# A gate on each unit's attention, a batch's rotation over two MLPs, and TensorE in written order up to the first MLP

## The chip, the cores and the metric

The kernel runs on one core of one Trainium2 chip, in float32. The metric is the device time of one execution in microseconds (us), the median of several runs. Engine names in the profile: PE is TensorE (PEld its weight loads), DVE VectorE, ACT ScalarE, POOL GpSimd, SP the engine that issues most DMAs.

## The reference

Two layers on `x` (8 batches, 512 tokens, 576 channels) with one conditioning row per batch. The first rotates each token in a 64-dimensional subspace: `U` from a QR of `P`, a rotation `R` from the matrix exponential of a skew matrix. The second is a transformer block whose attention runs over the 16 heads of each single token, not over tokens.

```python
U, _ = jnp.linalg.qr(P)
R = expm(skew(silu(cond) @ W.T + b))            # per batch, 64 x 64
z = x @ U
x = x + (z @ R - z) @ U.T

shift_a, scale_a, gate_a, shift_m, scale_m, gate_m = split(silu(c) @ ada_w + ada_b, 6)
qkv = modulate(layernorm(x), shift_a, scale_a) @ qkv_w + qkv_b      # 576 -> 3 * 576
attn = softmax(einsum('nthd,ntkd->nthk', q * 36**-0.5, k))          # 16 x 16 heads, per token
out = einsum('nthk,ntkd->nthd', attn, v).transpose(0, 2, 1, 3).reshape(n, t, d)
x = x + gate_a * (out @ proj_w + proj_b)
h = gelu(modulate(layernorm(x), shift_m, scale_m) @ fc1_w + fc1_b)  # 576 -> 2304
x = x + gate_m * (h @ fc2_w + fc2_b)
```

The transpose before the reshape mixes tokens: a tile of 128 tokens of attention becomes another set of rows for the projection, so attention goes out to DRAM (`att_d`) and comes back (`at`).

## The kernel before

Work is cut into 16 **units**: unit k is one batch and two of its four tiles of 128 tokens, `units[k] = (b, (0, 1))` or `(b, (2, 3))`.

A preparation of some 240 us computes the modulations, the QR and the exponential. Then these pieces follow one another for each unit:

- `rotation(b)` gives six pieces for a batch: `project_z(0)`, `rotate(0)`, `rotate(1)`, `project_z(1)`, `rotate(2)`, `rotate(3)`. `project_z` loads `xT`, multiplies it (`zps`, L730) and ScalarE copies it out; its first call also makes `gz`. `rotate` loads `xt`, multiplies (`rot`, L741), VectorE adds the product (L749), SP stores the result (`xr`), and `normed` computes the layernorm: statistics on VectorE (L137 to L139), the root on GpSimd (L140), the scaling on VectorE (L141).
- `feature_major(b, half)` transposes two normed tiles (`htr`, L773); ScalarE applies the modulation (`hT`, L777).
- `qkv(b, i)` gives six token groups of a tile: ten matmuls each (`qkvp`, L800), ScalarE's copy to `qs` (L811, three buffers) and ScalarE's DMA to `tok_d` (L812). The first two tiles stay on chip.
- `attention(b, ts)` is a generator, all on VectorE but the exponential: it loads the tokens (`qkv <- tok`, L825, three buffers), and for each tile forms the scores in four pairs of a product (L834) and a reduction (L841), subtracts the maximum, takes the exponential on ScalarE (L848), divides by the sum, and multiplies by the values in four more pairs (L862, L869). SP stores each tile to `att_d` (L871).
- `Projection`: SP loads weights, `at` (L902) and `x1`. `turn(t)` transposes `at` (`atr`, L913) and ScalarE copies it to `aT` (L914). `product(t, n)` multiplies (`pj`, L924); VectorE multiplies by the gate into `pt` (L926) and adds it (L927). `norm` is the second layernorm, `turn_normed` transposes (`h2tr`, L942) and ScalarE modulates (`h2T`, L945).
- `mlp`: nine groups of `fc1` (L969) with the gelu on ScalarE (L977), GpSimd's sums (`ss`, `s3`, L1025 to L1028) and the second layer's matmuls (L1040 to L1045), then `p7` (L1055), then VectorE's closing operations (L1065 to L1080, L984). A dictionary `aside` names pieces to be issued ahead of a group.

The main loop for unit k runs: the projection of unit k, with up to 12 token groups of a unit three ahead between its steps (`ahead`; two tiles per unit up to k = 10, then one); the MLP of unit k, with, for every first half of a batch, all six rotation pieces and both `feature_major` of batch b + 2 aside; then what is left of the attention of unit k + 1; and the generator for unit k + 2 is made.

What sets the order: outside `manual_schedule` a planner reorders each engine's instructions, by the program's order as priority and by its own estimate of when operands are ready, and then each engine works through its list in order. So VectorE may take up a later unit's attention as early as the planner saw its tokens, however late it stands in the program. The preparation has the written order on all engines. From there to the end of the first projection (`held`, closed at k = 0), GpSimd and VectorE have the written order, and TensorE, ScalarE and SP are planned. After that all are planned.

PSUM: `ps_mm` has two banks, shared by `zps`, `rot`, `htr`, `qkvp` and `pj`; `ps_f1` has two, for `fc1`, `atr`, `h2tr` and `p7`; `ps_acc` four.

Of the kernel before, what the change touches and what calls it, by code (L numbers as in the profile page):

```python
# [9 lines left out]
F32 = mybir.dt.float32  # L10
# [7 lines left out]
B, S, D = 8, 512, 576  # L18
R = 64
H, DH = 16, 36  # L20
# [4 lines left out]
HALF = D // 2  # L25
# [23 lines left out]
def rotate_then_dit_block(  # L49
# [16 lines left out]
    nc = tc.nc  # L66
# [36 lines left out]
    def srows(c):  # L103
        return 65 if c == 4 else 128
# [6 lines left out]
    small = ctx.enter_context(tc.tile_pool(name="small", bufs=4))  # L111
# [38 lines left out]
    engines = {mybir.EngineType.PE, mybir.EngineType.DVE, mybir.EngineType.Activation, mybir.EngineType.Pool}  # L150
    sc = const.tile([128, NK, B], F32, tag="sc", name="sc")
    with tc.manual_schedule(engines=engines), tc.tile_pool(name="prep", bufs=1) as prep, tc.tile_pool(name="qrs", bufs=2) as qrs, tc.tile_pool(
        name="ada", bufs=4
    ) as adap, tc.tile_pool(name="exs", bufs=1) as exs, tc.tile_pool(
        name="ps_qr", bufs=1, space=PSUM
    ) as ps_qr, tc.tile_pool(
        name="ps_ex", bufs=2, space=PSUM
    ) as ps_ex, tc.tile_pool(name="ps_m", bufs=2, space=PSUM) as ps_m, tc.tile_pool(
        name="ps_x", bufs=1, space=PSUM
# [374 lines left out]
        t, done = column_products(0), None  # L534
        for j in range(R):
            t, done = qr_step(j, t, done)
# [13 lines left out]
        if True:  # L550
# [131 lines left out]
            for h in range(2):  # L682
                p = slice(h * R, (h + 1) * R)
# [3 lines left out]
    tiles = ctx.enter_context(tc.tile_pool(name="tiles", bufs=2))  # L687
# [8 lines left out]
    def gate_rows(which, b):  # L696

        g = big.tile([128, D], F32, tag=f"gate{which}", name=f"gate_{which}_{b}")
        nc.sync.dma_start(out=g, in_=gates_d[which, b : b + 1, :].to_broadcast([128, D]))
        return g  # L700
# [86 lines left out]
    def qkv(b, i):  # L787


        hT = hTs[b]  # L790
        stay = b == 0 and i < 2
        if stay:
            tok = toks[b, i] = tiles.tile([128, 3 * D], F32, tag="qkv", name=f"qkv_{b}_{i}", bufs=3)

        def group(n):
            cols = slice(n * HALF, (n + 1) * HALF)
            ps = ps_mm.tile([128, HALF], F32, tag="mm", name=f"qkvp_{b}_{i}_{n}")
            for c in range(NK):
                k = srows(c)
                nc.tensor.matmul(  # L800
                    ps,
                    lhsT=hT[0:k, c, i * 128 : (i + 1) * 128],
                    rhs=wqkv[0:k, c, cols],
                    start=c == 0,
                    stop=c == NK - 1,
                )
            if stay:
                nc.scalar.copy(tok[:, cols], ps)
            else:
                qs = tiles.tile([128, HALF], F32, tag="qs", name=f"qs_{b}_{i}_{n}", bufs=3)  # L810
                nc.scalar.copy(qs, ps)  # L811
                nc.scalar.dma_start(out=tok_d[b][i * 128 : (i + 1) * 128, cols], in_=qs)  # L812

        return [lambda n=n: group(n) for n in range(6)]

    def attention(b, ts):


        HC = 4
        hb = f"{b}_{ts[0]}"  # L820
        own = []
        for i in ts:
            if (b, i) not in toks:
                toks[b, i] = tiles.tile([128, 3 * D], F32, tag="qkv", name=f"qkv_{b}_{i}", bufs=3)
                nc.sync.dma_start(out=toks[b, i], in_=tok_d[b][i * 128 : (i + 1) * 128])  # L825
            own.append(toks.pop((b, i)))
        sc = [small.tile([128, H, H], F32, tag="sc", name=f"sc_{hb}_{t}", bufs=3) for t in range(2)]

        def scores(t):
            q = own[t][:, 0:D].rearrange("p (h d) -> p h d", d=DH)  # L830
            k = own[t][:, D : 2 * D].rearrange("p (h d) -> p h d", d=DH)
            for c in range(H // HC):
                pr = tiles.tile([128, HC, H, DH], F32, tag="pr", name=f"qk_{hb}_{t}_{c}", bufs=1)
                nc.vector.tensor_tensor(  # L834
                    pr,
                    q[:, c * HC : (c + 1) * HC].unsqueeze(2).to_broadcast([128, HC, H, DH]),
                    k.unsqueeze(1).to_broadcast([128, HC, H, DH]),
                    ALU.mult,
                )
                yield  # L840
                nc.vector.tensor_reduce(sc[t][:, c * HC : (c + 1) * HC, :], pr, AX.X, ALU.add)  # L841
                yield

        def raised(t):
            mx = small.tile([128, H], F32, tag="mx", name=f"mx_{hb}_{t}", bufs=2)
            nc.vector.tensor_reduce(mx, sc[t], AX.X, ALU.max)
            nc.vector.tensor_tensor(sc[t], sc[t], mx.unsqueeze(2).to_broadcast([128, H, H]), ALU.subtract)
            nc.scalar.activation(sc[t], sc[t], AF.Exp, scale=DH**-0.5)  # L848

        def shares(t):  # L850
            sm = small.tile([128, H], F32, tag="sm", name=f"sm_{hb}_{t}", bufs=2)
            nc.vector.tensor_reduce(sm, sc[t], AX.X, ALU.add)
            nc.vector.reciprocal(sm, sm)
            nc.vector.tensor_tensor(sc[t], sc[t], sm.unsqueeze(2).to_broadcast([128, H, H]), ALU.mult)

        def values(t):
            i = ts[t]
            v = own[t][:, 2 * D :].rearrange("p (d h) -> p d h", h=H)
            att = tiles.tile([128, H, DH], F32, tag="att", name=f"att_{hb}_{t}")
            for c in range(H // HC):  # L860
                pr = tiles.tile([128, HC, DH, H], F32, tag="pr", name=f"pv_{hb}_{t}_{c}", bufs=1)
                nc.vector.tensor_tensor(  # L862
                    pr,
                    sc[t][:, c * HC : (c + 1) * HC, :].unsqueeze(2).to_broadcast([128, HC, DH, H]),
                    v.unsqueeze(1).to_broadcast([128, HC, DH, H]),
                    ALU.mult,
                )
                yield
                nc.vector.tensor_reduce(att[:, c * HC : (c + 1) * HC, :], pr, AX.X, ALU.add)  # L869
                yield  # L870
            nc.sync.dma_start(  # L871
                out=att_d[b][:, i * 128 : (i + 1) * 128, :].rearrange("h t d -> t h d"), in_=att
            )


        yield from scores(0)
        raised(0)
        yield from scores(1)
        raised(1)
        shares(0)  # L880
        yield from values(0)
        shares(1)
        yield from values(1)
# [206 lines left out]
    units = [(b, (i, i + 1)) for b in range(B) for i in (0, 2)]  # L1090
    N = len(units)

    def now(pieces):
        for piece in pieces:
            if piece:
                piece()

    def ops(n, of):
        for _ in range(n):
            next(of, None)  # L1100

    first, second = rotation(0), rotation(1)
    held = ctx.enter_context(ExitStack())
    held.enter_context(tc.manual_schedule(engines={mybir.EngineType.Pool, mybir.EngineType.DVE}))
    first[0]()
    feature_major(0, 0)
    q = qkv(0, 0)
# [6 lines left out]
    q = qkv(0, 1)  # L1114
    att = attention(*units[0])
# [31 lines left out]
    feature_major(1, 1)  # L1147
    now(qkv(1, 2))
    q = qkv(1, 3)
    now(q[:3])  # L1150
    ops(4, att)
    next_sums()
    ops(40, att)
# [1 line left out]
    att = attention(*units[1])  # L1155
    ops(6, att)

    ahead = {0: q[3:]}
    tiles_of = [(unit[0], i) for unit in units[4:] for i in unit[1]]
    for k in range(1, N - 1):  # L1160
        for tile_ in [tiles_of.pop(0) for _ in range(2 if k < 11 else 1)]:
# [3 lines left out]
    for k, (b, ts) in enumerate(units):  # L1165
        if ts[0] == 0:
            gate_a, gate_m = gate_rows(0, b), gate_rows(1, b)
            gb2 = big.tile([128, D], F32, tag="gb2", name=f"gb2_{b}")
            nc.sync.dma_start(out=gb2, in_=fc2_b.to_broadcast([128, D]))
            nc.gpsimd.tensor_tensor(gb2, gb2, gate_m, ALU.mult)  # L1170
        pr = Projection(b, ts, gate_a)
        q = ahead.get(k, [])
        if k:
            q = [piece for tile_ in q for piece in qkv(*tile_)]

        q = [None] * (12 - len(q)) + q
        now(q[:5])
        pr.turn(0)
        now(q[5:6])
        pr.product(0, 0)  # L1180
        pr.turn(1)
        now(q[6:7])
        pr.product(0, 1)
        pr.norm(0, gb2)
        now(q[7:8])
        pr.product(1, 0)
        now(q[8:9])
        pr.product(1, 1)
        pr.norm(1, gb2)
        if k == 0:  # L1190
            ops(1, att)
        now(q[9:11])
        pr.turn_normed((0, 1))
        now(q[11:])
        pr.turn_normed((2, 3))
        pr.turn_normed((4,))
        if k == 0:
            held.close()
        aside = {}
        if ts[0] == 0 and b + 2 < B:  # L1200
            p = rotation(b + 2)
            aside = {1: p[0], 2: p[1], 4: p[4], 5: p[5]}
            aside[3] = lambda two=p[2:4]: now(two)
            aside |= {7: lambda: feature_major(b + 2, 0), 8: lambda: feature_major(b + 2, 1)}
        mlp(pr, gate_m, aside)
        ops(40, att)
        if k + 2 < N:
            att = attention(*units[k + 2])


# [49 lines left out]
```

## Time and profile before

| | |
|---|---|
| median of 3 runs | 2232.36 us (2232.07 to 2233.22) |
| the profiled execution | 2232.94 us, span 2231.2 us |
| busy, share of the span | TensorE 94%, VectorE 81%, ScalarE 19%, GpSimd 31% |
| mean granted clock of TensorE | 0.956 |
| DMA | 400.79 MB, 180 GB/s in the mean |
| TensorE busy in 400 to 1300 us, per 100 us | 94.3 to 99.0 |
| VectorE busy in 400 to 1300 us, per 100 us | 94.6 to 99.4 |
| VectorE busy in 1700 to 2100 us, per 100 us | 45.5 to 64.4 |
| chain that ended last | TensorE 45%, VectorE 33%, issue 11% |

How to read it: a span is one execution from its first instruction to its last. Busy time of an engine counts instructions that run, its waits are listed apart, each put down to the one event that came last. Lines L... are those of the kernel before. The granted clock is 1 at full speed and 0.5 at half. The first 240 us are the preparation, where the clock is at half for long stretches; the change does not touch it.

### The profile page before, as it was taken

How to read it: one execution, taken by the hardware profiler on the slowest of the kernel's cores; microseconds unless marked ns; L12 is line 12 of the kernel's file. 1: busy time of each engine (PE TensorE's matmuls, PEld its weight loads, DVE VectorE, ACT ScalarE, POOL GpSimd, SP SyncE). 2: the span in 40 equal slices, each digit the busy share in tenths (PEclk: the TensorE clock that was granted, in tenths of full speed). 3: DMA queues.
4: the chain of work that ended last, by engine and by line, in shares of the span. 5: the costliest groups of instructions: out<-in, count | busy, mean ns of one | idle time of the engine just before them, and what ended most of it. 6: DMA issues, size and time to landing. Idle time of an engine off the chain costs nothing.

```text
span 2231.2 us, 27868 instructions
## 1 busy us (share of the span) xinstructions
PE 2099.5 (94%) x10087; PEld 1681.0 (75%) x10087; DVE 1812.8 (81%) x2530; ACT 428.2 (19%) x916; POOL 687.8 (31%) x918
## 2 busy tenths in 40 slices
PE   6996998999999999999999998999999999999988
PEld 3475776787878787787778787887878788887867
DVE  8898598799999999999999997979879526742930
ACT  2232221212121121212122121212122111111110
POOL 2331233332324133333324132322313323332422
PEclk9855898999999999999999999999999999999999
DMA  8202365483848567575657566575756665765654
GB/s 268 84 2 73 101 210 141 148 265 126 262 143 256 161 188 216 163 214 178 206 177 236 157 188 190 192 208 168 206 186 198 196 209 185 206 206 177 198 175 125
DMA packets 239789, 400.79 MB, mean 180 GB/s; under 512 B 85502, under 2 KB 127435, under 8 KB 239652
## 3 DMA queue, kind: packets, MB, share of 16 engines
q1 hardware_dynamic: 213732, 372.46, 55.1%
q10 hardware_dynamic: 25920, 26.55, 3.7%
q8 instruction: 80, 1.31, 0.2%
q14 instruction: 57, 0.47, 0.1%
HBM read 340.01 MB, written 58.94 MB: 179 GB/s over the span
## 4 chain that ended last, share of the span: by engine, by line
PE 45%; DVE 33%; issue 11%; POOL 5%; DMA 3%; ACT 2%; SPq 0%; ACTq 0%; POOLq 0%; DVEq 0%
PE fc L969 15%; PE qkvp L800 8%; DVE pv L862 6%; DVE att L869 6%; DVE qk L834 6%; DVE sc L841 6%; PE fc L1040 5%; PE fc L1045 3%; PE pj L924 3%; PE fc L1042 2%; PE p L1055 2%; DMA qkv<-tok 1%; PE ada L352 1%; PE zps L730 1%; PE dp L270 1%
## 5 line engine op out<-in xcount | busy, mean ns | idle before, releaser
L969 PE MATMUL fc<-h2T,w 128*128 128x256 f32 (+1 forms) x2880 | 652.7, 381 | 7.3 <-ACT h2T L945 7.1
L969 PEld LDWEIGHTS fc<-h2T,w 128*128 128x128 f32 (+1 forms) x2880 | 539.6, 191 | 83.4 <-ACT h2T L945 12.1
L800 PE MATMUL qkvp<-wqkv,hT 128*128 128x288 f32 (+1 forms) x1920 | 490.8, 409 | 7.0 <-ACT qs L811 4.4
L800 PEld LDWEIGHTS qkvp<-wqkv,hT 128*128 128x128 f32 (+1 forms) x1920 | 362.5, 191 | 109.7 <-ACT qs L811 6.2
L834 DVE TENSOR_TENSOR qk<-qkv 128x2304 f32<-128x2304 f32 x128 | 334.5, 2613 | 70.4 <-DMA qkv<-tok 62.0
L862 DVE TENSOR_TENSOR pv<-sc,qkv 128x2304 f32<-128x2304 f32 x128 | 335.2, 2618 | 2.2
L1025 POOL TENSOR_TENSOR ss<-gt 128x128 f32<-128x128 f32 x144 | 133.7, 929 | 637.8 <-ACT gt L977 637.8
L869 DVE TENSOR_REDUCE att<-pv 128x144 f32<-128x2304 f32 x128 | 325.7, 2545 | 2.5
L841 DVE TENSOR_REDUCE sc<-qk 128x64 f32<-128x2304 f32 x128 | 325.7, 2544 | 2.1
L977 ACT ACTIVATE gt<-fc 128x512 f32<-128x512 f32 x144 | 86.0, 598 | 652.5 <-PE fc L969 652.2
L811 ACT COPY qs<-qkvp 128x288 f32<-128x288 f32 x180 | 71.9, 400 | 531.4 <-PE qkvp L800 489.6
L1045 PEld LDWEIGHTS fc<-wt,ss 128*128 128x128 f32 x1152 | 161.6, 191 | 15.3
L1040 PE MATMUL fc<-wq,gt 128*128 128x288 f32 x576 | 163.4, 405 | 2.8 <-ACT gt L977 2.8
L1045 PE MATMUL fc<-wt,ss 128*128 128x144 f32 x1152 | 165.6, 287 | 0.0
L140 POOL TENSOR_TENSOR rstd_m<-rstd_m,mhalf 128x1 f32<-128x1 f32 x32 | 30.6, 956 | 357.6 <-DVE rstd_m L139 353.6
L1040 PEld LDWEIGHTS fc<-wq,gt 128*128 128x128 f32 x576 | 107.5, 189 | 26.4 <-ACT gt L977 3.7
L1071 DVE TENSOR_TENSOR u<-u,fc 128x288 f32<-128x288 f32 x16 | 7.2, 449 | 147.9 <-ACT u L1070 146.8
L924 PE MATMUL pj<-w2q_p,aT 128*128 128x288 f32 x384 | 110.1, 424 | 17.3 <-DVE pt L926 12.7
L1027 POOL TENSOR_TENSOR ss<-gt,ss 128x128 f32<-128x128 f32 x144 | 109.0, 757 | 11.2
L985 POOL TENSOR_TENSOR x<-x,mt 128x288 f32<-128x288 f32 x64 | 51.0, 797 | 187.7 <-DVE mt L984 187.7
L924 PEld LDWEIGHTS pj<-w2q_p,aT 128*128 128x128 f32 x384 | 73.1, 195 | 43.8 <-DVE pt L926 17.2
L926 DVE TENSOR_TENSOR pt<-pj,gate 128x288 f32<-128x288 f32 x64 | 28.8, 450 | 91.0 <-PE pj L924 91.0
(253 smaller groups left out, 2416.6 us busy)
## 6 DMA issues: line engine op xcount, KB each, us to landing
w<-in_fc_w SPq DMA_DIRECT2D x288, 320.0 KB
wq<-in_fc_q SPq DMA_DIRECT2D x144, 432.0 KB
wt<-comb_d SPq DMA_DIRECT2D x144, 432.0 KB
tok<-qs ACTq DMA_DIRECT2D x180, 144.0 KB
qkv<-tok SPq DMA_DIRECT2D x30, 864.0 KB
w2q_p<-in_proj_w SPq DMA_DIRECT2D x32, 432.0 KB
xT<-in_x_t SPq DMA_DIRECT2D x16, 640.0 KB
xt<-in_x SPq DMA_DIRECT2D x32, 288.0 KB
```

Source lines behind the costliest of these rows:

```text
L800: nc.tensor.matmul(ps, lhsT=hT[0:k, c, i * 128 : (i + 1) * 128], rhs=wqkv[0:k, c, cols], start=c == 0, stop=c == NK - 1,)
L834: nc.vector.tensor_tensor(pr, q[:, c * HC : (c + 1) * HC].unsqueeze(2).to_broadcast([128, HC, H, DH]), k.unsqueeze(1).to_broadcast([128, H ...
L841: nc.vector.tensor_reduce(sc[t][:, c * HC : (c + 1) * HC, :], pr, AX.X, ALU.add)
L862: nc.vector.tensor_tensor(pr, sc[t][:, c * HC : (c + 1) * HC, :].unsqueeze(2).to_broadcast([128, HC, DH, H]), v.unsqueeze(1).to_broadcast( ...
L869: nc.vector.tensor_reduce(att[:, c * HC : (c + 1) * HC, :], pr, AX.X, ALU.add)
L924: nc.tensor.matmul(ps, lhsT=aT[0:k, c, :], rhs=w, start=c == 0, stop=c == NK - 1)
L969: nc.tensor.matmul(ps[:, k], lhsT=w1[0:n, c, :], rhs=h2T[0:n, c, 0 : NU * 128], start=c == 0, stop=c == NK - 1,)
L977: nc.scalar.activation(gt.rearrange("p k t s -> p (k t s)"), ps.rearrange("p k s -> p (k s)"), AF.Gelu)
L1025: nc.gpsimd.tensor_tensor(ss[:, 0], gt[:, 0, 1], gt[:, 1, 1], ALU.add)
L1027: nc.gpsimd.tensor_tensor(ss[:, 2], gt[:, 1, 0], ss[:, 1], ALU.subtract)
L1040: nc.tensor.matmul(p[k], lhsT=whole[k][0], rhs=whole[k][1], start=g == 0, stop=stop)
L1045: nc.tensor.matmul(bank[:, side], lhsT=lhs, rhs=rhs[:, n * QUARTER : (n + 1) * QUARTER], start=False, stop=stop, skip_group_check=True,)
```

## The change

- `attention` takes a function `after`; if there is one, the first VectorE instruction of the unit's attention copies one column of what it returns into the first score tile. The loop hands over `pr.aT[0]`. The function is called when the generator first runs, one turn of the loop later, so `pr` is then the projection of the unit before: attention of unit j reads `aT[0]` of unit j - 1. This holds from unit 2 on.
- The six rotation pieces of batch b + 2 and its two `feature_major` are shared by the MLPs of the two units of batch b, three and one in each, before groups 1, 3, 5 and 8.
- `held` includes TensorE, which has the written order until the end of the first projection. The last tile's token groups before the loop are two, not three, and those in the first projection are placed one by one.
- `qs` has four buffers in place of three, `sc` two in place of three.

```diff
-                qs = tiles.tile([128, HALF], F32, tag="qs", name=f"qs_{b}_{i}_{n}", bufs=3)
+                qs = tiles.tile([128, HALF], F32, tag="qs", name=f"qs_{b}_{i}_{n}", bufs=4)
...
-    def attention(b, ts):
+    def attention(b, ts, after=None):
...
-        sc = [small.tile([128, H, H], F32, tag="sc", name=f"sc_{hb}_{t}", bufs=3) for t in range(2)]
+        sc = [small.tile([128, H, H], F32, tag="sc", name=f"sc_{hb}_{t}", bufs=2) for t in range(2)]
+
+        if after is not None:
+            nc.vector.tensor_copy(sc[0][:, 0, 0:1], after())
...
-    held.enter_context(tc.manual_schedule(engines={mybir.EngineType.Pool, mybir.EngineType.DVE}))
+    held.enter_context(tc.manual_schedule(engines={mybir.EngineType.PE, mybir.EngineType.Pool, mybir.EngineType.DVE}))
...
     q = qkv(1, 3)
-    now(q[:3])
+    now(q[:2])
...
-    ahead = {0: q[3:]}
+    ahead = {0: [None] * 5 + q[2:3] + [None] * 3 + q[3:]}
...
         aside = {}
-        if ts[0] == 0 and b + 2 < B:
-            p = rotation(b + 2)
-            aside = {1: p[0], 2: p[1], 4: p[4], 5: p[5]}
-            aside[3] = lambda two=p[2:4]: now(two)
-            aside |= {7: lambda: feature_major(b + 2, 0), 8: lambda: feature_major(b + 2, 1)}
+        if b + 2 < B:
+            if ts[0] == 0:
+                coming = rotation(b + 2)
+            p = coming[:3] if ts[0] == 0 else coming[3:]
+            aside = {1: p[0], 3: p[1], 5: p[2], 8: lambda: feature_major(b + 2, ts[0] // 2)}
         mlp(pr, gate_m, aside)
         ops(40, att)
         if k + 2 < N:
-            att = attention(*units[k + 2])
+            att = attention(*units[k + 2], after=lambda: pr.aT[0][:, 0, 0:1])
```

## The prediction

> **What bounds the kernel.** I read the page's busy line first, then busy time in stretches cut where TensorE starts `turn` of each unit (T0 to T15, from the timeline: T0 368, T1 510, T2 625, T11 1735, T12 1833, T13 1932, T14 2030, T15 2129), then the waits, then the timeline around TensorE's largest gaps.
>
> ```profile
> span 2231.2 us, 27868 instructions
> PE 2099.5 (94%) x10087; PEld 1681.0 (75%) x10087; DVE 1812.8 (81%) x2530; ACT 428.2 (19%) x916; POOL 687.8 (31%) x918
> ```
> ```profile
> 1257.00:1368.00 111.00, 111.00 (x525) 92.24 (x524) 109.56 (x70) 20.38 (x38) 32.48 (x40) 1.00 0.66 193
> 1368.00:1502.00 134.00, 126.75 (x582) 102.56 (x581) 108.91 (x115) 27.23 (x51) 41.63 (x53) 0.97 0.65 198
> 1735.00:1833.00 98.00, 96.40 (x462) 80.84 (x461) 35.03 (x45) 15.15 (x28) 28.28 (x44) 1.00 0.66 204
> ```
> After the stretch, columns are its length, then busy time of PE, PEld, DVE, ACT, POOL, then the granted clock. From 400 us on TensorE never rests long, whether VectorE is full (111) or a third full (98), so it sets the end. No matmul is added or removed; all there is to win is TensorE's gaps. Added up from the timeline (over 0.3 us), they are 50 us between 400 and 2120, and 17 us between 344 and 369.
>
> ```profile
> PE pj L924 <- DVE pt L926: 12.7, 9, 4.6
> PE fc L1042 <- POOL ss L1027: 7.0, 6, 2.5
> PE atr L913 <- DMA at<-att: 6.0, 2, 5.2
> PE zps L730 <- DVE xt L749: 5.7, 4, 3.2
> DVE qk L834 <- DMA qkv<-tok: 62.0, 7, 13.0
> ```
> Columns: total us, times, longest. The last line explains part of the first. From unit 7 on VectorE has caught up with its supply: it starts a unit's attention as soon as the projection stage three units ahead has made its tokens, and stands in front of their load. What is queued behind it stands too, such as `pt`, which must empty the PSUM bank that TensorE wants next (VectorE, then TensorE, at unit 10's projection):
>
> ```profile
> 1621.67 0.46 DVE L137 BATCH_NORM_STATS2 st_m<-x 128x6 f32<-128x288 f32 x1
> 1629.07 2.56 DVE L834 TENSOR_TENSOR qk<-qkv 128x2304 f32<-128x2304 f32 x1 [6.94 <-DMA qkv<-tok]
> 1631.54 0.45 DVE L926 TENSOR_TENSOR pt<-pj,gate 128x288 f32<-128x288 f32 x1
> ```
> ```profile
> 1632.05 3.25 PE L924 MATMUL pj<-w2q_p,aT 128*128 128x288 f32 x6 [3.63 <-DVE pt L926]
> 934.85 4.64 PE L730 MATMUL zps<-xT,u 128*128 128x256 f32 x10 [3.23 <-DVE xt L749]
> 348.82 5.17 PE L800 MATMUL qkvp<-wqkv,hT 128*128 128x288 f32 x10 [4.07 <-ACT qs L811]
> 368.24 0.90 PE L913 MATMUL atr<-ident,at 128*128 128x128 f32 x3 [5.23 <-DMA at<-att]
> ```
> A gap costs more than itself: six `pj` matmuls took 3.25 us here, 1.62 elsewhere, because the clock fell to half:
>
> ```profile
> 931.00:945.00 14.00, 10.77 (x38) 8.53 (x37) 12.83 (x13) 2.25 (x3) 1.40 (x4) 0.76 0.52 167
> 1628.00:1641.00 13.00, 8.88 (x25) 6.05 (x24) 11.90 (x11) 0.80 (x2) 0.31 (x1) 0.74 0.30 91
> ```
> Ten matmuls after the gap took 4.96 us, start to start, against 2.43: 2.5 per drop. There are four in mid-kernel: after gaps of 3.24, 3.63 and 4.60, and after 2.08 and 2.28 that lie 2 us apart. [...]
>
> **Part 1, the gate.** A unit's attention may start only when the unit before it has `aT[0]`. It binds everywhere: even the latest starter was early (unit 2's attention began at 487.5, T1 was 510).
> - Removed: the head-of-line wait for tokens. They are now made two units before use. The gaps of 4.60 (1388) and 3.63 (1628) go, with 2 x 2.5 of clock: -13. What is late next is the ordinary `pt` wait behind one 2.55 us attention operation (0.3 to 1.2 us in units 1 to 3), which was there already.
> - Moved: the two exponentials of a unit. In before they drift to the end of an MLP, where the change of ScalarE's table (1.28 us, twice) holds up the last gelu: gaps at 1102 to 1107 (0.68 + 2.49) and 1231 to 1237 (2.08 + 2.28 + 2.3 of clock), and three of 0.5 to 0.7. After the gate they sit some 25 and 50 us behind `turn`, in the projection and the first MLP groups, where TensorE has a group queued. 11.7 at stake; I take -8 (bounds -11.7 and +3, if the early groups pay what three ends of MLPs paid).
> - Added: 14 copies of 128x1; nearest row 0.15 us (`rstd`, 128x1). On VectorE, outside TensorE's chain: 2 us of slack. Behind the waiting copy are queued attention and `pt`; `pt` needs a product that TensorE computes after that same `aT`, so no one else waits.
> - Added: VectorE loses its lead. From `aT[0]` to the attention's end it needs 16 pairs of 5.19 us (83.0), the softmax steps 4.3 and the projection's own operations 7.6, so 95; the last MLP's closing operations push its start to about +3. At the end of the kernel a store and a load hand it over: last reduce done 2128.86, `turn(1)` 2137.65, so 8.8. Ready: 3 + 95 + 1 of joints + 8.8 = 107.8 after `turn`. TensorE comes to `turn(1)` after its own period plus 6 (turn 1.1, two products 4.9). Units 1 to 11 have a period of 122.5 ((1735 - 510) / 10); with half a rotation (5.2) the attention is ready at 113, wanted at 128.5: covered. Units 12 and 13 have 98.4: wanted at 104.4, late by 3.4 plus 2.3 of clock, unless its six token groups (2.43 each) are ordered ahead. Bounds 0 and +11.4; I take +6. Unit 15 does not change: its second tile is made at k = 14 in both (loaded 2065.6).
>
> **Part 2, the shared rotation.** `project_z(1)` no longer follows a `rotate` in the same MLP, where both PSUM banks still waited for VectorE's `xt`: gaps 1.52, 0.77 and 3.24 and 2.2 of clock, 7.7; I take -7. Each MLP now gets one x load, two `rotate` and one `feature_major`; the four x and xr DMAs of a half are spread on SP's queue, and the two normed tiles are held from group 3 to 8, against four before. Tokens for the next batch are still made one unit after `feature_major`. Bounds -7.7 and +3 (an early `rotate` that waits for its load).
>
> **Part 3, TensorE in written order until the first MLP, and four `qs`.** The planned order is nearly the written one up to 362 us. Then the planner put `turn(0)` of unit 0 ahead of nine token groups, and it waited 5.23 us, at half clock until 372. Written: five transposes, eight groups, `turn(0)`, one group, `product(0, 0)`. From 361.9 to 394.9 lie 33 us; the work at full clock is 22 for nine groups, 3 for transposes and 1 for the turn, so 26: -7. The next three products have no groups between them, as now (394.9 to 405, no gap). `turn(1)` needs the second tile, ready at about 378 by the 8.8 above, wanted at about 388. The fourth `qs` puts off the stall at 344.8 by one group, 2.43, if its cause (ScalarE stood 8 us in front of a store) stays; -1 of it. Smaller `sc` costs nothing: in-order VectorE has finished with the old tile first. Together -8 (bounds -17, all gaps there; +5, a written instruction that waits where the planner had a filler).
>
> **Sum.** -13 - 8 + 6 - 7 - 8 = -30. Counted another way: units 1 to 3 show what a projection loses when nothing special happens, 3.1, 4.2 and 2.3. Fifteen units at 2.5 make 37 where now 50 and 9 of clock are lost: -22, with the start and the late units -24. I take -28. The profiled execution took 2232.9 (1.7 more than its span; 0.6 above the median): 2204.9, less the 0.6: **2204**.
>
> **Rivals.**
> - *The gate comes too late (slower).* If VectorE's order puts the copy behind the projection's last norm, some 25 us after `turn`, attention is ready 22 us later. Units 12 and 13 then wait 25 us each and 2.3 of clock, the ten others about 1.5 and some clock (20): +75, with -34 of gains: about 2270. It decides once attention starts more than 15 us after `aT[0]`. For: the projection is earlier in the program. Against: at units 1 to 3 attention pairs are planned between the projection's operations. 13%.
> - *The gaps move (no change).* Now every projection coincides with a starting attention; if each loses unit 2's 4.2 us, 14 make 59, all that was removed; the start's -8 goes against the late units' +6: 2222 to 2240, middle 2231. For: a new plan is drawn for everything after the first projection. 19%.
> - *The start loses*: written order waits 5 us, the rest holds: 2217. 5%.
> - *Cleaner than thought*: all units like 7 and 9 (0 and 1.4): 2180. 10%.
> - *GpSimd is blocked.* Its `s` takes 0.456 us in the median and 2.85 at most, when a VectorE product runs. Late MLPs, now free of attention, get it: up to 2.4 a group, nine groups, units 11 to 14: +86, 2290. A saturated MLP (unit 1's) lost only 0.65 to it, so 3%. [...]
> - That the gate never binds is excluded by the 487.5 above.
>
> **Numbers.** The forecast (2192 to 2222) has 50%. A measurement here can tell about 0.2%, 4.5 us. Faster: 50 + 10 + 5 + 5 of "the gaps move" = 70%; same 8; slower 13 + 3 + 6 = 22. The range 2184 to 2246 leaves out half of the cleaner case, most of the late gate and GpSimd: 19%.
>
> **What would show it.** Right: `qk <- DMA qkv<-tok` under 20 us; no `pj` gap over 2 us; no `zps <- xt`; `at<-att` at the first `turn` gone; attention starting within 5 us of each `aT[0]`; VectorE near 95% busy in 1735 to 2030. Wrong: gaps of over 5 us ahead of `turn(1)` at units 13 and 14, `atr <- DMA at<-att` growing to tens of us, new half-clock stretches, or TensorE waits before 400 us that were not there.

## The result, and the profile after

| | before | after |
|---|---|---|
| median, runs of the same chip | 2232.79 us (2232.07 to 2239.58) | 2208.88 us (2205.87 to 2213.21) |
| profiled execution, span | 2232.94, 2231.2 us | 2205.87, 2204.2 us |
| mean granted clock | 0.956 | 0.961 |

The ratio is 0.9888, 95% interval [0.9862, 0.9913]: faster by 1.1%. Line numbers below are those of the kernel after, or of an experiment's own kernel; in the kernel after, most lines stand 4 further down than before.

The page's span, busy line and the new group of copies:

```profile
span 2204.2 us, 27929 instructions
PE 2090.5 (95%) x10087; PEld 1679.3 (76%) x10087; DVE 1801.2 (82%) x2544; ACT 434.9 (20%) x922; POOL 714.1 (32%) x918
L831 DVE COPY sc<-aT 128x1 f32<-128x1 f32 x14 | 2.1, 152 | 109.4 <-ACT aT L918 109.4
```

TensorE has as many instructions as before and is busy 9 us less, at a mean clock of 0.961 for 0.956. The 14 copies cost 2.1 us and wait 109.4 us. The waits show where:

```profile
DVE sc L831 <- ACT aT L918: 109.4, 10, 11.0
DVE qk L838 <- DMA qkv<-tok: 8.6, 1, 8.6
PE qkvp L800 <- DVE pt L930: 15.0, 14, 1.8
PE h2tr L946 <- DVE xm L141: 6.4, 5, 3.5
PE fc L1046 <- POOL ss L1031: 3.2, 6, 0.9
PE atr L917 <- DMA at<-att: 2.8, 1, 2.8
```

Ten of the 14 copies wait, 11 us each; the other four, of units 12 to 15, don't. The wait for tokens is down from 62.0 us to 8.6, `zps` no longer waits for `xt`, and no `pj` waits for `pt`. That last wait has not gone but moved: it is now `qkvp` that meets it, 14 times, 1.8 us at most.

In stretches (after length, busy time of PE, PEld, DVE, ACT, POOL, then granted clock), one middle unit and one late one:

```profile
1095.00:1215.00 120.00, 118.18 (x554) 96.48 (x553) 98.45 (x89) 24.06 (x45) 39.95 (x47) 1.00 0.66 193
1788.00:1893.00 105.00, 100.50 (x462) 82.97 (x461) 95.63 (x75) 17.95 (x31) 32.47 (x45) 0.97 0.67 189
```

In the middle TensorE lost 1.8 of 120 us, with VectorE idle for 21.55. In the late unit, unit 12, it lost 4.5 of 105, and VectorE is at 91%. In the same unit before, TensorE lost 1.6 of 99, and VectorE was at 75% (36% in units 11 and 13):

```profile
1833.00:1932.00 99.00, 97.40 (x468) 81.53 (x467) 74.38 (x60) 15.16 (x28) 33.51 (x44) 1.00 0.66 199
```

To see where the 27.0 us of the two spans came from, I cut both at the starts of the MLPs (first `fc<-h2T` of each unit in the timeline). Stretch k runs from the start of MLP k to that of MLP k + 1 and so holds the projection of unit k + 1. Gaps are TensorE's, over 0.3 us:

| stretch | before | after | difference | gaps before, after |
|---|---|---|---|---|
| start to MLP 0 | 414.9 | 412.0 | -3.0 | 11.3, 11.6 (from 240 us) |
| 0 to 9 | 1243.2 | 1195.1 | -48.1 | 43.8, 14.0 |
| 10 to 14 | 493.5 | 517.2 | +23.7 | 13.7, 25.0 |
| MLP 15 to the end | 79.6 | 80.0 | +0.4 | none |

The middle won 48 us. 30 are gaps. Some 11 are clock: four half-clock stretches of 6.8 us, in which TensorE was busy for 21.7 us in all, half of it lost. 3.2 are no gain: two `rotate` pieces, 8 matmuls (`rot`) of 0.41 us, lie in stretches 0 to 9 before and in 10 to 14 after. The other 4 I can't place; gaps under 0.3 us changed by 0.5 only. The late units gave half of it back: without the two pieces, 20.5 of 44.9 us.

### The profile page after: what moved, and what is told of

It reads as the page before. It is cut to its first block, busy times and chain, and to the rows that moved or that the text cites. A ratio compares the mean times of both kernels' runs of the same rounds, so it can differ in the third digit from the quotient of the medians.

```text
span 2204.2 us, 27929 instructions
## 1 busy us (share of the span) xinstructions
PE 2090.5 (95%) x10087; PEld 1679.3 (76%) x10087; DVE 1801.2 (82%) x2544; ACT 434.9 (20%) x922; POOL 714.1 (32%) x918
## 4 chain that ended last, share of the span: by engine, by line
PE 66%; issue 13%; DVE 9%; POOL 4%; DMA 4%; ACT 3%; SPq 0%; ACTq 0%; POOLq 0%; DVEq 0%
PE fc L973 28%; PE fc L1044 9%; PE qkvp L800 8%; PE fc L1049 6%; PE fc L1046 3%; PE p L1059 2%; PE pj L928 1%; ACT h2T L949 1%; DMA out<-x 1%; DVE sc L845 1%; PE zps L730 1%; PE dp L270 1%; DMA gate<-gates_d 1%; PE ada L352 1%; PE htr L773 1%
## 5 line engine op out<-in xcount | busy, mean ns | idle before, releaser
L973 PEld LDWEIGHTS fc<-h2T,w 128*128 128x128 f32 (+1 forms) x2880 | 542.1, 192 | 83.6 <-ACT h2T L949 11.6
L800 PE MATMUL qkvp<-wqkv,hT 128*128 128x288 f32 (+1 forms) x1920 | 494.1, 412 | 23.6 <-DVE pt L930 15.0
L1029 POOL TENSOR_TENSOR ss<-gt 128x128 f32<-128x128 f32 x144 | 155.0, 1076 | 548.3 <-ACT gt L981 548.3
L866 DVE TENSOR_TENSOR pv<-sc,qkv 128x2304 f32<-128x2304 f32 x128 | 330.4, 2581 | 1.8
L140 POOL TENSOR_TENSOR rstd_m<-rstd_m,mhalf 128x1 f32<-128x1 f32 x32 | 19.6, 613 | 439.4 <-DVE rstd_m L139 369.8
L928 PE MATMUL pj<-w2q_p,aT 128*128 128x288 f32 x384 | 104.2, 406 | 0.9 <-ACT aT L918 0.9
L1046 PE MATMUL fc<-wq,ss 128*128 128x288 f32 x288 | 94.1, 408 | 3.2 <-POOL ss L1031 3.2
L1030 POOL TENSOR_TENSOR ss<-ss,gt 128x128 f32<-128x128 f32 x144 | 95.9, 666 | 0.0
L1044 PE MATMUL fc<-wt,gt 128*128 128x288 f32 x288 | 93.4, 406 | 0.0
L831 DVE COPY sc<-aT 128x1 f32<-128x1 f32 x14 | 2.1, 152 | 109.4 <-ACT aT L918 109.4
```

The source lines that it names most:

```text
L800: nc.tensor.matmul(ps, lhsT=hT[0:k, c, i * 128 : (i + 1) * 128], rhs=wqkv[0:k, c, cols], start=c == 0, stop=c == NK - 1,)
L866: nc.vector.tensor_tensor(pr, sc[t][:, c * HC : (c + 1) * HC, :].unsqueeze(2).to_broadcast([128, HC, DH, H]), v.unsqueeze(1).to_broadcast( ...
L928: nc.tensor.matmul(ps, lhsT=aT[0:k, c, :], rhs=w, start=c == 0, stop=c == NK - 1)
L973: nc.tensor.matmul(ps[:, k], lhsT=w1[0:n, c, :], rhs=h2T[0:n, c, 0 : NU * 128], start=c == 0, stop=c == NK - 1,)
L1029: nc.gpsimd.tensor_tensor(ss[:, 0], gt[:, 0, 1], gt[:, 1, 1], ALU.add)
L1030: nc.gpsimd.tensor_tensor(ss[:, 1], ss[:, 0], gt[:, 0, 0], ALU.subtract)
```

## The experiments

**Each part alone, and the change without its gate.** Four kernels, compared with the kernel before.

`gate_only` is the kernel before with:
```diff
-    def attention(b, ts):
+    def attention(b, ts, after=None):
...
+        if after is not None:
+            nc.vector.tensor_copy(sc[0][:, 0, 0:1], after())
...
-            att = attention(*units[k + 2])
+            att = attention(*units[k + 2], after=lambda: pr.aT[0][:, 0, 0:1])
```


> The kernel before with the gate alone (rotation, written order and buffers as before). Between the first MLP's start and the thirteenth's, the changed kernel is 37 us faster than before, and from there to the last MLP's start 13 us slower. Theory of mechanisms: of the 37 the gate holds about 29 (token wait, pt, late exponentials), the rotation about 8; the gate alone gives 2232 - 29 + 13, about 2216, with no wait of qk on tokens beyond 15 us and waits of the same size in every unit. Rival, unequal periods: with all six rotation pieces in one MLP the gated attention does not fit its unit, and every second projection waits: 2228 or slower. Rival, new plan: any edit draws another order, gaps stay irregular from unit to unit, time anywhere in 2220 to 2245.

`rot_only` is the kernel before with the change's `aside` (three pieces and one `feature_major` in each of two MLPs), nothing else.

> The kernel before with the shared rotation alone. Theory of mechanisms: only the gaps of zps on xt go (7.7 us), token waits and late exponentials stay: about 2225, pj gaps of over 3 us still there. Rival, equal periods: the even load is what makes the changed kernel regular, and most of the 37 us come with it: 2205 or less. Rival, new plan: 2220 to 2245 with the gaps at other places.

`written_only` is the kernel before with PE in `held`, `q[:2]`, the placed groups, four `qs` and two `sc`.

> The kernel before with TensorE in written order up to the first MLP, the token groups placed one by one, four qs and two sc. The changed kernel starts its first MLP 3 us earlier than before. Theory of mechanisms: those 3 us and nothing else: 2229, with steady gaps as before. Rival, new plan: what follows is drawn anew and moves by 10 us either way: 2219 to 2239.

`no_gate` is the kernel after with:
```diff
-            att = attention(*units[k + 2], after=lambda: pr.aT[0][:, 0, 0:1])
+            att = attention(*units[k + 2])
```


> The changed kernel without the gate (shared rotation, written order, four qs, two sc). Theory of mechanisms: 29 us of steady gaps come back, 13 us of the late units go: 2209 + 16, about 2225, with qk waiting on tokens for tens of us again. Rival, equal periods: the regular pattern stays without the gate and the late loss goes: 2196. Rival, new plan: no regular pattern, 2215 to 2240.

| | ratio to before, 95% | start to MLP 0 | stretches 0 to 9 | 10 to 14 |
|---|---|---|---|---|
| before | 1 | 414.9 | 1243.2 | 493.5 |
| gate_only | 0.9928 [0.9907, 0.9949] | 410.6 | 1197.8 | 520.4 |
| rot_only | 0.9999 [0.9988, 1.0011] | 412.0 | 1238.4 | 492.8 |
| written_only | 1.0007 [0.9994, 1.002] | 419.7 | 1240.6 | 494.1 |
| no_gate | 0.9983 [0.9968, 0.9998] | 412.1 | 1243.7 | 494.7 |
| after | 0.9888 [0.9862, 0.9913] | 412.0 | 1195.1 | 517.2 |

The gate makes both halves of the result, the 45 us won in the middle and the 27 us lost late (in each, 3.2 are again the two `rotate` pieces). The two other parts are worth nothing alone and 4 us together, with an interval that only just leaves out 1. The waits of `gate_only` against those of `no_gate`:

```profile
DVE sc L830 <- ACT aT L917: 89.9, 10, 10.9
DVE qk L837 <- DMA qkv<-tok: 8.6, 1, 8.6
PE qkvp L800 <- DVE pt L929: 14.9, 14, 1.8
```
```profile
DVE qk L838 <- DMA qkv<-tok: 63.6, 7, 13.0
PE pj L928 <- DVE pt L930: 18.6, 9, 6.9
```

With the gate VectorE's wait for tokens goes; without it the wait is as long as ever, whatever else of the change is there.

**The shared rotation where the gate is there.** `no_rot` is the kernel after with the kernel before's `aside`, all six pieces in one MLP; `after_again` is the kernel after once more; `no_gb2` leaves out GpSimd's addition of the second bias (L936) and serves a later question (its output lacks that bias).

> The changed kernel with all six rotation pieces in one MLP again (gate, written order and buffers stay). With the gate alone the two periods of a batch were 126.0 and 113.0, together 239.0; in the changed kernel 120.0 and 118.8, together 238.8. Theory: sharing is worth nothing in the middle and 4 to 6 us around the twelfth MLP, where the half rotation lengthens a short unit: 0.991 to 0.993. Rival, written order is what sets the gate alone (0.9928) apart from the change (0.9888): this run stays at 0.989.

> The changed kernel as it is, to stand beside the others on one chip: 0.989 of before.

`no_rot` came to 0.9895 [0.9867, 0.9924], `after_again` to 0.9886 [0.9856, 0.9916]. `no_rot`'s MLPs alternate (126.0 and 113.0 us, 239.0 a pair), after's hardly do (120.0 and 118.8, 238.8 a pair). The sharing evens the units out; it doesn't shorten them. Stretches are of one execution each. 0 to 9 and 10 to 14 repeat well (1195.1 and 1195.0, 517.2 and 517.3 in after and `after_again`), the start doesn't (412.0 and 414.3), and totals of single executions scatter: `no_rot`'s profiled one, 2205.95 us, is 10 us under its other three. `no_rot` and `gate_only` are alike to 0.1 us in stretches 0 to 9 and 0.7 in 10 to 14; their profiled executions differ by 3.0 us at the start, which is all that the written order and the four `qs` can have brought, and within the scatter of that stretch (below).

**Is it the tokens, the place or the wait?** `gate_lag2` lets a unit's attention start one unit earlier, at the turn of the unit before the last:
```diff
+            if t == 0:
+                self.mark = small.tile([128, 1], F32, tag="mark", name=f"mark_{self.hb}", bufs=3)
+                nc.scalar.copy(self.mark, aT[:, 0, 0:1])
...
-            att = attention(*units[k + 2], after=lambda: pr.aT[0][:, 0, 0:1])
+            att = attention(*units[k + 2], after=lambda pr=pr: pr.mark)
```


> The changed kernel with the gate one unit earlier: attention of unit j waits for the turn of unit j - 2 (through a copy of one column on ScalarE). In the changed kernel VectorE idles 11 us at the gate per unit, so this gate does not bind until about unit 11: attention is not tied to the projection, and yet never runs into tokens that are not made. Theory of the lock (the gain comes from attention standing at a fixed place in each projection): units 1 to 11 lose 4 us each again as in the kernels without the gate, late part 290 to 295: 2209 + 25 - 10, about 2222. Rival, tokens: the gain is that VectorE no longer stands in front of token loads: middle as in the changed kernel, late part recovered: 2198.

It came to 0.9901 [0.9875, 0.9926], and split itself in two. In its first four stretches the copies wait for nothing, since VectorE has still to earn the lead; from stretch 4 to 9 they wait 11.2 us each. One copy and one stretch of either kind:

```profile
555.04 0.14 DVE L831 COPY sc<-mark 128x1 f32<-128x1 f32 x1
993.78 0.15 DVE L831 COPY sc<-mark 128x1 f32<-128x1 f32 x1 [11.18 <-ACT mark L922]
```
```profile
497.00:620.00 123.00, 118.25 (x551) 97.50 (x550) 120.98 (x102) 22.07 (x44) 35.64 (x47) 0.99 0.64 195
992.00:1110.00 118.00, 116.66 (x550) 96.26 (x549) 99.27 (x89) 23.44 (x44) 41.58 (x47) 1.00 0.67 204
```

Where the copy does not wait, VectorE is never idle, gaps are 4.7, 4.7, 4.1 and 4.4 us and periods 125.4, 123.9, 125.4, 122.1; there is no wait for tokens among them. Where it waits, gaps are 0.5 to 1.5 and periods 118.5 to 120.2. So the tokens were not the main thing: a saturated VectorE costs 4 to 5 us a unit without them. The first forecast holds for the four units that are not tied and fails for the six that are; the second fails for those four.

**The lead for the late units.** Two kernels drop the gate from some unit on, so that VectorE can run ahead before the late, shorter units.

```diff
-            att = attention(*units[k + 2], after=lambda: pr.aT[0][:, 0, 0:1])
+            att = attention(*units[k + 2], after=(lambda: pr.aT[0][:, 0, 0:1]) if k + 2 <= 8 else None)
```


> The gate for units 2 to 8 only; from unit 9 on VectorE can gain some 11 us on TensorE per unit. Theory of overlap: late part falls to 293 to 298 (a lead of 40 us at unit 13), units 9 to 12 run unlocked and lose 2 to 3 us more each; total within 5 us of the changed kernel. Rival, lead pays all: late part 290, middle unchanged, 12 us less. Rival, lock: units 9 to 12 return to 4 us of gaps and more, late part no better: 10 us more.

> The changed kernel with the gate for units 2 to 11 only; 12 to 15 start as soon as VectorE is free. The late units (thirteenth MLP start to the last) take 302 us in the changed kernel, 289.5 before. Theory of overlap: they lose because attention now runs across their short projections, and three units of lead are gone; 10 us of lead does not change that: late part 297 to 302, total 0 to 5 us less than the changed kernel. Rival, the gate's own wait: the late loss is VectorE standing at the gate; without it 290, total 12 us less.

`gate_to8` came to 0.9885 [0.9857, 0.9913], `gate_to11` (with 11 for 8) to 0.9909 [0.9883, 0.9936]. Against after, `gate_to8` took 10.8 us longer in stretches 0 to 9 (1205.9, all of it from 7 on) and 11.6 us less in 10 to 14 (505.6). With the gate gone at unit 9, the lost lead comes back, and each unit that earns it pays with gaps of 2.9 to 4.0. `gate_to11` frees VectorE too late: stretch 12, of 111.6 us, has one gap of 6.79 us (`h2tr` for `xm`), and stretches 12 to 14 took 306.0 us, more than either forecast.

**A lead earned by degrees.** `ramp` puts the signal that opens a unit's attention a little earlier at each of units 3 to 8 (for unit j behind group 8, 6, 4, 2 and 0 of the MLP of unit j - 2, then behind its `h2T`) and at the turn of unit j - 2 from unit 9 on:

```diff
+    SIGNAL = {3: 8, 4: 6, 5: 4, 6: 2, 7: 0, 8: 'h2T', 9: 'turn', 10: 'turn', 11: 'turn', 12: 'turn', 13: 'turn', 14: 'turn', 15: 'turn'}
```


> The changed kernel with the gate moved ahead step by step, by 7 to 38 us per unit: unit 2 waits for the turn of unit 1 as before, units 3 to 7 for gelu 8, 6, 4, 2 and 0 of the MLP before that, unit 8 for the first h2T of unit 6, units 9 to 15 for the turn of unit j - 2 (ScalarE copies one column at that place and VectorE waits for the copy). Theory of the lock (what counts is that each unit's attention starts at an event of TensorE, wherever it lies): periods of 118.5 to 120.5 in all units up to the twelfth MLP, and the lead gained gives the late part back, 289 us in place of 302 to 305: 13 us less than the changed kernel, 0.983 of before. Rival, the place counts (start of the projection is the good one): units 3 to 8 lose 4 us each as when unlocked, and the total is that of the changed kernel or of the gate with lag two, 0.989 to 0.990.

It came to 0.9861 [0.9842, 0.988], the lowest ratio of all; its interval overlaps after's, so no gain over the change is shown. The late units cost 508.2 us (after 517.2), but stretches 0 to 9 cost 1210.7: gaps are 2.2 to 4.1 in stretches 1 to 6, and periods of up to 125.0 make the first theory a miss. In 2 to 5 VectorE does wait, for 2 to 10 us, but not at a turn. Waiting alone isn't enough, then. In stretches 7 to 9, with waits of 11.2 us at the turn, gaps are 0.5, 1.5 and 0.5.

**Making VectorE wait at the turn.** `ramp_meet` is ramp with a copy of one column of `aT[0]` into the first `pt` tile at each unit's first turn, ahead of the projection's own VectorE work.

> The kernel is ramp (signals set ahead of the attention of the last unit by a few groups at units 3 to 7, at the turn of the unit before the last from unit 9) with one more thing: at each unit's first turn VectorE copies one column of the finished attention tile aT[0] into the first `pt` tile, so that it meets TensorE right ahead of every projection. Theory "meeting" (what counts is that VectorE stands and waits for TensorE right ahead of the projection, so that the written interleaving is met on the chip): the gaps of units 3 to 7, 2.5 to 4.1 us in ramp at periods of 121.3 to 125.0, fall to 1 to 1.7 us, the periods to about 119.5, and the time to about 10 us less than ramp's, ratio about 0.981. Rival "place" (VectorE has no slack in those units, or it is the place where attention stands that costs; one more wait only adds a stall): the periods stay at 121 to 125 or grow, ratio 0.986 or higher.

It came to 0.9883 [0.9864, 0.9903] with gaps of 3.4, 2.3, 3.5, 4.9, 2.9 and 2.8 in stretches 1 to 6: the first theory's forecast is a miss. The trace shows why. The copy never waited in those units, because VectorE came to it late. VectorE of `ramp_meet` at unit 6's projection, then TensorE, then VectorE of the kernel after at the same unit's:

```profile
1112.43 0.14 DVE L928 COPY pt<-aT 128x1 f32<-128x1 f32 x1
1112.55 2.56 DVE L866 TENSOR_TENSOR pv<-sc,qkv 128x2304 f32<-128x2304 f32 x1
1115.14 2.55 DVE L873 TENSOR_REDUCE att<-pv 128x144 f32<-128x2304 f32 x1
1117.61 0.45 DVE L944 TENSOR_TENSOR pt<-pj,gate 128x288 f32<-128x288 f32 x1
```
```profile
1118.11 2.07 PE L939 MATMUL pj<-w2q_p,aT 128*128 128x288 f32 x6 [2.90 <-DVE pt L944]
```
```profile
1096.80 0.15 DVE L831 COPY sc<-aT 128x1 f32<-128x1 f32 x1 [10.94 <-ACT aT L918]
1096.99 2.55 DVE L845 TENSOR_REDUCE sc<-qk 128x64 f32<-128x2304 f32 x1
1099.58 2.56 DVE L838 TENSOR_TENSOR qk<-qkv 128x2304 f32<-128x2304 f32 x1
1102.05 0.45 DVE L930 TENSOR_TENSOR pt<-pj,gate 128x288 f32<-128x288 f32 x1
```

Up to here the order is the same in both: the copy, two attention operations, the first `pt`, 5.2 us behind the copy. What differs is the phase. After, the copy starts as ScalarE's `aT` ends. In `ramp_meet` ScalarE's copies to `aT` began at 1107.66 and took 0.75, so VectorE is 4.0 us late; `pt` is as much later, and TensorE stands for 2.90. A wait makes no phase where the engine arrives late.

Behind the first `pt` these two orders differ. `ramp` itself has a cleaner pair: in its units 7 and 8 the 21 VectorE operations from the copy to the fourth `pt` are the same in the same order (buffer names aside), and so are the first 90 matmuls from the turn on. VectorE's copy and first `pt` and TensorE's second product, in unit 7 (turn at 1229.00) and then in unit 8 (turn at 1350.00):

```profile
1233.36 0.14 DVE L831 COPY sc<-mark 128x1 f32<-128x1 f32 x1
1238.60 0.45 DVE L938 TENSOR_TENSOR pt<-pj,gate 128x288 f32<-128x288 f32 x1
1239.11 1.72 PE L936 MATMUL pj<-w2q_p,aT 128*128 128x288 f32 x6 [1.55 <-DVE pt L938]
```
```profile
1351.87 0.15 DVE L831 COPY sc<-mark 128x1 f32<-128x1 f32 x1 [11.19 <-ACT mark L894]
1357.12 0.45 DVE L938 TENSOR_TENSOR pt<-pj,gate 128x288 f32<-128x288 f32 x1
1358.39 1.62 PE L936 MATMUL pj<-w2q_p,aT 128*128 128x288 f32 x6
```

In unit 7 VectorE came late, 4.4 us behind the turn, and the copy had nothing to wait for; in unit 8 it came early, waited, and went on 1.9 us behind the turn. The first `pt` is 9.6 and 7.1 us behind the turn. TensorE stood for 1.55 and, one product later, 0.54 us in unit 7, and not at all before these products in unit 8. With the same order, then, the time at which VectorE comes to the turn makes the gaps.

The projections of units 1 to 10 in all 14 profiles say the same. In 81 of them VectorE had stood at the turn for over 5 us, waiting for ScalarE's copy; there TensorE's gaps from the turn to the MLP are 0.5 to 1.4 us. In the 59 others they are 0 to 8.4, 3.2 in the mean. What counts is that VectorE comes to the turn early, with its slack there and not elsewhere.

**The late units: GpSimd?** Behind the late loss stand waits at short projections under attention. TensorE, in a middle unit and then in late ones:

```profile
1119.30 5.12 PE L800 MATMUL qkvp<-wqkv,hT 128*128 128x288 f32 x20 [0.78 <-DVE pt L930]
1704.49 5.12 PE L800 MATMUL qkvp<-wqkv,hT 128*128 128x288 f32 x20 [1.79 <-DVE pt L930]
1811.59 6.81 PE L800 MATMUL qkvp<-wqkv,hT 128*128 128x288 f32 x20 [1.79 <-DVE pt L930]
1819.51 0.87 PE L946 MATMUL h2tr<-ident,xm 128*128 128x128 f32 x6 [1.10 <-DVE xm L141]
```

The same gap before `qkvp` is 1.0 us longer late, and here the 20 matmuls behind it took 6.81 us, not 5.12, with the granted clock at 0.50 from 1812.3 to 1815.3. Ahead of it, GpSimd and VectorE:

```profile
1807.36 1.40 POOL L936 TENSOR_TENSOR x<-x,gb 128x576 f32<-128x576 f32 x1 [0.69 <-DVE xm L141]
```
```profile
1807.56 3.61 DVE L838 TENSOR_TENSOR qk<-qkv 128x2304 f32<-128x2304 f32 x1
1811.10 0.45 DVE L930 TENSOR_TENSOR pt<-pj,gate 128x288 f32<-128x288 f32 x1
```

The product took 3.61 us where it takes 2.55; it started 0.20 after GpSimd's addition, and `pt` stood behind it. The times fit a product that stood until the addition was done: 2.55 behind the addition's end at 1808.76 is 1811.31, and the product ended at 1811.17. `no_gb2` takes the addition away:

> The changed kernel without GpSimd's addition of the second bias to x1 in the norm (the output lacks that bias). In the late units a score product of VectorE took 3.61 us in place of 2.55 while that addition ran, and the pt behind it came so much later: TensorE's gap is 1.79 there and 0.78 in earlier units. [...] Rival, order: the gap of 1.79 is the plan's order, and stays.

Its one execution took 2208.06 us. The product took 2.54 and the gap before `qkvp` fell to 0.72, so the longer product came with the addition. But the next gap grew, `h2tr` for `xm` to 2.57:

```profile
1814.90 5.12 PE L800 MATMUL qkvp<-wqkv,hT 128*128 128x288 f32 x20 [0.72 <-DVE pt L930]
1822.60 0.92 PE L945 MATMUL h2tr<-ident,xm 128*128 128x128 f32 x6 [2.57 <-DVE xm L141]
```

Stretches 12 to 14 took 301.9 us (after 302.1, before 289.5), 10 to 14 took 514.5 (after 517.2), and half-clock stretches are still there (6.8 us at 1823, 3.4 at 1929 and 2031). So GpSimd explains that one gap and at most some 3 us, not the loss: VectorE has no slack left in these units, and the wait moves to its next operation.

## Why the prediction came out right, point by point

The time was right (2204 against 2208.88, in the range of the forecast), by steps of which two were far off in opposite directions: the middle won 17 us more than forecast, and the late units lost 14.5 us more. That they cancelled is luck.

**The sum of the middle** (-13, -8 and -7: -28) was 17 us too small (44.9 without the two `rotate` pieces). The mechanism, attention bound to the turn, was right; its size was not. The step that failed is the second count's floor, "units 1 to 3 show what a projection loses when nothing special happens", 2.5 each (the 3.1, 4.2 and 2.3 are gaps of whole units; their projections alone lose 2.5, 2.6 and 2.3). These units too had a saturated VectorE, and after the gate stretches 0 to 9 lose 14.0 in ten, 1.4 each.
- *The head-of-line wait, -13.* The waits went as said (62.0 to 8.6). But `gate_lag2` loses 4 to 5 us per unit without any wait for tokens, so I read these two gaps as the worst cases of a VectorE that comes late; that they are was not shown by itself.
- *The exponentials, -8.* No `fc` matmul waits for a gelu (`gt`) any more, against 2.8 us in two waits, and the longest wait for `ss` fell from 2.5 to 0.9. The exponentials sit in the projection and the first groups, as said; the clock's fall near 1234 is gone with them (granted 0.69 in 1231 to 1242 before, 1.00 in 1225 to 1245 after). No experiment parts this term from the rest.
- *What is late next*, "the ordinary `pt` wait ... 0.3 to 1.2", was right: 0.78 in the middle.
- *The shared rotation, -7.* Mis-sized: nothing measurable, 0.9999 [0.9988, 1.0011] alone and none beside the gate. The gaps named (`zps` for `xt`) do go, but in `rot_only` TensorE's gaps add up to 69.3 against 68.8 before: they come back as `pj` for `pt` (15.3 against 12.7) and `h2tr` for `xm` (11.5 against 7.6).

**The start, -8**, was mis-sized: -3.0 in after, and `written_only` reached its first MLP 4.8 us later than before. The 5.23 us wait of `turn(0)` went, as said. But the stall of the fourth `qs`, one of 4.07 us, became two of 1.99 and 2.78 (after) or three of 2.0 (`written_only`), all behind `qs`. The start of MLP 0 lies between 406.4 and 419.7 in the profiled executions of kernels whose preparation is the same, so single executions can't resolve it better. The bound of -17 was wrong as well: the gaps over 0.3 us between 344 and 369 add up to 10.3, and the half clock lasted until 374, not 372.

**The lost lead, +6**, was mis-sized and its place wrong. It had the attention of the late units "wanted at 104.4, late by 3.4 plus 2.3 of clock" at `turn(1)`. Attention 13 ended at 1880.3, 13 us ahead of unit 13's turn and 92.2 behind unit 12's; with the prediction's own 8.8 that is 101, not 107.8. Some 2.6 of this come from the planner, which let the first score product slip ahead of the copy (1777.35, the copy at 1790.05), since that product writes `pr` (`qk` in the profile) and only the reduction needs `sc`. What was lost, 23.7 us in stretches 10 to 14, is the two `rotate` pieces (3.2), 11.3 us more of gaps, among them the waits shown above, and half-clock stretches of 3.4 us at 1812, 1822, 1918, 1928 and 2030 that before had not, five times 1.7. `gate_to8`, `gate_lag2` and `ramp` win back 9 to 14 us of it by having VectorE ahead, and lose it where it gets ahead.

**The rivals.** "The gate comes too late" did not occur: copies of the middle units start with `aT[0]`. "The gaps move" is what the rotation and the late units did, each on its own, but not the middle. "GpSimd is blocked": the longest of its first sums (`ss`, L1029) took 2.78 us, and TensorE waited 3.2 us for `ss` in all (7.0 before); as a bound it didn't occur, but the reverse, a VectorE product longer beside a GpSimd addition (3.61 us for 2.55), did.

**What would show it.** Right: tokens under 20 us, no `pj` gap, no `zps` for `xt`, the wait at the first `turn` gone, the copies right behind `aT[0]`. VectorE was 91% busy in 1735 to 2030 (267.69 of 295), not 95. Two of the signs of being wrong came too: half-clock stretches in the late units, and waits of TensorE before 400 us that were not there (1.22 us at 317, 1.36 at 367).

## What to carry to other kernels

Where two engines pass small tiles to and fro and one of them has long filler work, the order on paper held on the chip, here, only where that engine reached the meeting point early and waited there; a 0.15 us copy that depends on the other engine's first result can bring this about, as long as the engine has slack to spend (here 7 to 11 us in 120). Where it has none, the copy does nothing: look at busy time by stage first, and expect the gain of the slack stages to be partly paid back in the tight ones. And two parts that each remove a named gap may be worth nothing, since another wait behind the same busy engine takes its place; only the sum of all gaps in the stretch tells.

## What the runs showed of the hardware

- TensorE's clock fell after short gaps, and not always. Four late units of after have the same gap of 1.79 us before the same 20 matmuls; these took 5.12, 6.81, 6.81 and 5.12 us. Behind the gap of 0.78 to 0.80 there in units 1 to 10 they took 5.12 every time, and the falls at 1822, 1928 and 2030 followed two or three gaps of 0.5 to 1.1 us close together. The five late half-clock stretches of after are 3.41 us long each and start 10.24, 95.57, 10.24 and 102.40 us apart, which is 3, 28, 3 and 30 times 3.413; the four in mid-kernel before are 6.83 each. What decides between a fall and none after the same gap was not shown.
- A VectorE product that started 0.20 us after a GpSimd addition took 3.61 us where it takes 2.55, 1.06 more; without that addition it took 2.54.
